# A two-layer graph network on one core: halves of the adjacency matrix fetched and compared at other places of the batch, mirrored blocks first fetched two units sooner

## The chip, the core and the metric

The kernel runs on one core of a Trainium2 chip. The metric is the time of one execution on the device, in microseconds. A run of the kernel before takes 3390.76 us (median of three runs: 3390.57, 3390.76 and 3401.56). Profiles are of one execution each.

## The reference

For 16 graphs of 1024 nodes with 256 features, two layers are computed. Each begins with a layer norm and a ReLU, and each is added to its input:

```
h = relu(layernorm(x));  x = x + L0(h, adj)
h = relu(layernorm(x));  x = x + L1(h, adj)

L0: qkv = layer_norm(h) in 8 heads of 32;  scores = qkv qkv^T / sqrt(32)
    attn = softmax(where(adj > 0, scores, -inf));  h = h + attn qkv
    return h + gelu(layer_norm(h) W1 + b1) W2 + b2
L1: p = h W;  logits = p a_1 + (p a_2)^T + (p a_12) p^T
    e = where(adj > 0, leaky_relu(logits), -9e15)
    return elu(h W_1 + softmax(e) h W_2)
```

Queries, keys and values of L0 are one and the same tensor, so the scores are symmetric. The adjacency matrix is of 32-bit integers and symmetric with ones on the diagonal; the kernel makes use of the symmetry, and it also tests it while it runs.

## The kernel before

All the work is in `fast_path`; `general_path` runs only if a test at the end says so, which is not the case here. A batch is one graph. Nodes are cut into 8 tiles of 128 and into two halves of 512 (`qh` 0 and 1); the 8 heads into two groups of four (`g`).

**Attention of a batch** (`attention`, L984) goes in units. A unit is one group of heads, one half of the queries and one tile of keys. TensorE makes the scores (`s`, L1010), VectorE adds the mask (L1023, two halves of 128x1024), ScalarE takes the exponential and sums it (L1030), and in the next unit TensorE weighs the values (`o`, L1125). For batches from 1 on, 16 units with `qh` 0 come first, then 8 with `qh` 1. For half of the first 16 units, `mirror` (L1040) keeps what the symmetry gives: VectorE transposes the exponentials by 32x32 blocks into `x` (L1046; `xp` has one buffer), SyncE writes them to a DRAM tile `blocks` (L1053), GpSimd adds up their sums (`add_up`, L1059), and SyncE writes these to `rows` (L1074). `gather` (L1084) brings the sums back. In the 8 later units, which this document calls the mirrored stretch, `weigh_mirrored` (L1107) uses 16 blocks that `fetch` (L1093) has read back from DRAM; there are two halves of one buffer (`em`), and block k + 2 is fetched when block k has been used. `em` shares its buffer with the hidden layer `hid` of chunks 0 and 3. Batch 0 computes all 32 units and mirrors nothing.

**Masks.** For each half of a batch, `turn_masks` (L904) loads four row tiles of the adjacency matrix (`fetch_mask`, L587, two loads of 256 KB each into the two buffers `adj`). VectorE converts them to fp8 (`convert_mask`, L594) into `mq`, which has one buffer, and SyncE transposes them by DMA into `mk` (L917; five buffers). `compare_masks` (L924) is the test of symmetry: GpSimd subtracts a part of `mq` from a part of `mk` (`odd`, L932, 4 times for half 0 and 8 times for half 1), and ScalarE squares the difference and sums it into `uneven` (L941). At the end these sums have to be zero.

**The rest of the batch** (`rest`, L1246) is the MLP (`ph`, `po`) and layer 1 (`puT`, `pg`, `lg`, `pa`, `pf`), all by `matmul`, which cuts each product into four column strips (L574) except near the end (L571). The rest of batch b runs between the attention units of batch b + 1. `prologue` (L789) loads and normalizes the next batch.

**What sets the order.** The program is written out in one order by cooperating generators: `stream_a` (attention), `stream_b` (rest), `stream_p`, `stream_c` (prologue), `stream_m` (masks, L1626) and `stream_s`. Each yields a place, a number whose whole part is the batch, and the one with the lowest place goes next. In batches from 1 on a unit with `qh` 0 is 1/25.2 of a batch wide, one with `qh` 1 1.15/25.2. `spread(pieces, n, start, end)` puts pieces at even distances between two places. Beside that, `defer(us, f)` puts a step off until a clock, which counts estimated TensorE time, has advanced by that much. Each engine, and SyncE as the queue of all these DMAs, takes its instructions in the order in which they were written out.

Of the kernel before, what the change touches and what calls it, by code (L numbers as in the profile page):

```python
# [14 lines left out]
AF = mybir.ActivationFunctionType  # L15
ALU = mybir.AluOpType
# [479 lines left out]
def fast_path(  # L496
# [28 lines left out]
    nc = tc.nc  # L525
# [4 lines left out]
    NG = H // GH  # L530
    NT = N // P
# [4 lines left out]
    TPH = QW // P  # L536
# [123 lines left out]
    uneven = const.tile([P, B * 3 * TPH], F32, name="uneven")  # L660
# [111 lines left out]
    def defer(us, f):  # L772
        deferred.append((clock[0] + us, len(deferred), f))

        return clock[0] + us
# [128 lines left out]
    def turn_masks(b, qh, st):  # L904

        ts = list(range(qh * TPH, (qh + 1) * TPH))
        raw = fetch_mask(b, ts[0])
        yield
        m = mkp.tile([P, NT // 2, QW, 2], FP8, tag="mk", name=f"mk_{b}_{qh}")
        st[qh] = m  # L910
        pairs = m.rearrange("p m q r -> p m (q r)").bitcast(BF16)
        mq = st["mq", qh] = mqp.tile([P, TPH, N], FP8, tag="mq", name=f"mq_{b}_{qh}")
        convert_mask(mq[:, 0], *raw)
        raw = fetch_mask(b, ts[1])
        for i in range(TPH):
            yield
            nc.sync.dma_start_transpose(pairs[:, :, i * P : (i + 1) * P], mq[:, i].bitcast(BF16))  # L917
            if i + 1 < TPH:
                convert_mask(mq[:, i + 1], *raw)
            if i + 2 < TPH:  # L920
                raw = fetch_mask(b, ts[i + 2])


    def compare_masks(b, qh, st):  # L924

        for half in range(qh + 1):
            for i in range(TPH):
                kt = qh * TPH + i
                odd = tmpp.tile([P, QW], BF16, tag="w1", bufs=6, name=f"odd_{b}_{qh}_{half}_{i}")
                key = st[half][:, kt // 2, :, kt % 2]  # L930
                query = st["mq", qh][:, i, half * QW : (half + 1) * QW]
                nc.gpsimd.tensor_tensor(  # L932
                    odd.rearrange("p (u v x) -> p u v x", u=2, v=2),
                    key.rearrange("p (u v x) -> p u v x", u=2, v=2),
                    query.rearrange("p (u x v) -> p u v x", u=2, v=2),
                    op=ALU.subtract,
                )
                n = (b * 3 + qh + half) * TPH + i
                defer(
                    3.0,  # L940
                    lambda odd=odd, n=n: nc.scalar.activation(odd, odd, AF.Square, accum_out=uneven[:, n : n + 1]),  # L941
                )
                yield
        if (b, qh) == (B - 1, NQH - 1):
            defer(
                4.0,
                lambda: nc.vector.tensor_reduce(
                    seen[:, 4:5], uneven, axis=mybir.AxisListType.X, op=ALU.add
                ),
            )  # L950
# [33 lines left out]
    def attention(b, st):  # L984
# [6 lines left out]
        blocks = {}  # L991
# [48 lines left out]
        def mirror(g, kt, es):  # L1040
            x = xp.tile([P, NT // 2 * GH, GH, HD], F32, tag="x", name=f"x_{b}_{g}_{kt}")
            if g not in blocks:
                blocks[g] = dramp.tile([NT // 2 * GH, NT // 2 * GH, HD, P], F32, tag=f"blocks{g}", name=f"blocks_{b}_{g}")

            def turn(i):
                nc.vector.transpose(  # L1046
                    x[:, :, 2 * i : 2 * i + 2, :].rearrange("p c h j -> p h c j"),
                    es[i].rearrange("p h (c i) -> p h c i", i=HD),
                )

            def write():
                for a in range(GH):
                    nc.sync.dma_start(  # L1053
                        blocks[g][(kt - TPH) * GH + a].rearrange("c i e -> i c e"),
                        x[a * HD : (a + 1) * HD].rearrange("p c h j -> p c (h j)"),
                    )

            def add_up():
                add = lambda out, p, q: nc.gpsimd.tensor_tensor(out, p, q, op=ALU.add)  # L1059
                part = denp.tile([P, TPH * GH, GH, 8], F32, tag="part", bufs=1, name=f"part_{b}_{g}_{kt}")  # L1060
                add(part, x[:, :, :, 0:8], x[:, :, :, 8:16])
                add(part, part, x[:, :, :, 16:24])
                add(part, part, x[:, :, :, 24:32])
                add(part[:, :, :, :4], part[:, :, :, :4], part[:, :, :, 4:])
                add(part[:, :, :, :2], part[:, :, :, :2], part[:, :, :, 2:4])
                row = denp.tile([P, GH, TPH, GH], F32, tag="row", name=f"row_{b}_{g}_{kt}")
                add(
                    row.rearrange("p a t h -> p t a h"),
                    part[:, :, :, 0].rearrange("p (t a) h -> p t a h", a=GH),
                    part[:, :, :, 1].rearrange("p (t a) h -> p t a h", a=GH),  # L1070
                )
                if ("rows", g) not in blocks:
                    blocks["rows", g] = dramp.tile([TPH, P, GH * TPH * GH], F32, tag=f"rows{g}", name=f"rows_{b}_{g}")
                defer(7.0, lambda: nc.sync.dma_start(blocks["rows", g][kt - TPH], row.rearrange("p a t h -> p (a t h)")))  # L1074

            defer(1.5, lambda: turn(0))
            defer(3.5, lambda: turn(1))
            defer(5.5, write)
            defer(6.5, add_up)

        def gather(g):
# [84 lines left out]
        for n, u in enumerate(units):  # L1166
            qh, g, kt = u
            make_turns()
            es, rest_of_weights = scores(*u)
            go_on()  # L1170
            rest_of_weights()
            first = n == 0 or units[n - 1][:2] != u[:2]
            last = n == len(units) - 1 or units[n + 1][:2] != u[:2]
            scored.append((weigh, (*u, es, first, last)))
            if not mirrored:
                if qh == NQH - 1 and kt % TPH == TPH - 1:
                    invert(kt // TPH, g)
                    if kt < NT - 1:
                        close(kt // TPH, g)
                yield 1.0  # L1180
                continue
            if qh == 0:
                if kt >= TPH:
                    mirror(g, kt, es)
                if n == NG * NT - 1:
                    defer(2.0, lambda: fetch(0))
                    defer(2.2, lambda: fetch(1))
                if n == NT + 1:
                    gather(0)
                if n == NT + 3:  # L1190
                    invert(0, 0)
                    close(0, 0)
                yield 1.0
                continue
            if n == NG * NT + 1:
                gather(1)
            if n == NG * NT + 3:
                invert(0, 1)
                close(0, 1)
            if last:  # L1200
                invert(1, g)
            widths = ((0.8, 0.3, 0.05), (0.5, 0.45, 0.2), (0.4, 0.45, 0.3), (0.3, 0.5, 0.35))[kt - TPH]
            yield widths[0]
            weigh_mirrored(k)
            yield widths[1]
            weigh_mirrored(k + 1)
            k += 2
            yield widths[2]

    def go_on():  # L1210
        if scored:
            f, args = scored.pop()
            f(*args)
        clock[0] += 2.0
# [340 lines left out]
    def spread(pieces, n, start, end):  # L1555
        yield start
        for i, _ in enumerate(pieces):
            yield start + (end - start) * (i + 1) / n

    states = [{} for _ in range(B + 1)]  # L1560
# [65 lines left out]
    def stream_m():  # L1626
        for b in range(B):
            if b:
                start, end = (b - 0.28, b - 0.10) if b == 1 else (b - 0.43, b - 0.25)
                yield from spread(turn_masks(b, 0, states[b]), 5, start, end)  # L1630
                yield from spread(compare_masks(b, 0, states[b]), TPH, end + 0.01, end + 0.09)
                yield from spread(turn_masks(b, 1, states[b]), 5, b + 0.03, b + 0.2)
                yield from spread(compare_masks(b, 1, states[b]), 2 * TPH, b + 0.21, b + 0.36)
            else:
                yield from spread(compare_masks(b, 0, states[b]), TPH, b + 0.02, b + 0.2)
                yield from spread(turn_masks(b, 1, states[b]), 5, b + 0.23, b + 0.43)
                yield from spread(compare_masks(b, 1, states[b]), 2 * TPH, b + 0.52, b + 0.7)
# [85 lines left out]
```

## Time and profile before

| | before |
|---|---|
| median of three runs | 3390.76 us |
| the profiled execution | 3397.68 us |
| its span | 3395.4 us |
| TensorE busy (mean granted clock 0.988) | 3239.8 us, 95% |
| VectorE busy | 2584.0 us, 76% |
| ScalarE busy | 2205.2 us, 65% |
| GpSimd busy | 1515.3 us, 45% |
| TensorE waiting for `em`, at L1107 | 64.5 us |
| the ACTIVATE of L941: 192 times, mean | 625 ns |
| L932: 192 times, mean | 1165 ns |
| L594: 248 times, mean | 562 ns |

In the views of the profile PE is TensorE, PEld its loading of weights, DVE VectorE, ACT ScalarE, POOL GpSimd and SP SyncE. Busy time is the time in which at least one instruction of an engine ran. A wait is the idle time of an engine just before an instruction, named after what ended it. A line is the line of the kernel; a helper's line stands for all its callers, so tiles are given too. A group is all instructions of one line, operation and tile; "x240" is how many there were. A window is a piece of the span, in microseconds from its start.

### The profile page before, as it was taken

How to read it: one execution, taken by the hardware profiler on the slowest of the kernel's cores; microseconds unless marked ns; L12 is line 12 of the kernel's file. 1: busy time of each engine (PE TensorE's matmuls, PEld its weight loads, DVE VectorE, ACT ScalarE, POOL GpSimd, SP SyncE). 2: the span in 40 equal slices, each digit the busy share in tenths (PEclk: the TensorE clock that was granted, in tenths of full speed). 3: DMA queues.
4: the chain of work that ended last, by engine and by line, in shares of the span. 5: the costliest groups of instructions: out<-in, count | busy, mean ns of one | idle time of the engine just before them, and what ended most of it. 6: DMA issues, size and time to landing. Idle time of an engine off the chain costs nothing. (4 is left out here: it accounts for less than half of the span.)

```text
span 3395.4 us, 114970 instructions
## 1 busy us (share of the span) xinstructions
PE 3239.8 (95%) x48866; PEld 1600.2 (47%) x48866; DVE 2584.0 (76%) x4881; ACT 2205.2 (65%) x5384; POOL 1515.3 (45%) x1757
## 2 busy tenths in 40 slices
PE   6899999999999999999999999999999999999998
PEld 2244445444444444444444454444544444444477
DVE  5677787777888778787787887778877787877734
ACT  6875756758567585665757567585675856758553
POOL 3563543635436364453635436354362543636120
PEclk9999999999999999999999999999999999999999
DMA  5256454454654455555455544645445464444410
GB/s 136 69 112 141 114 134 128 102 150 116 141 131 109 131 120 133 132 119 128 109 147 123 135 121 110 150 115 136 126 104 141 114 144 127 109 130 113 119 36 14
DMA packets 741161, 404.82 MB, mean 119 GB/s; under 512 B 173217, under 2 KB 699937, under 8 KB 740641
## 3 DMA queue, kind: packets, MB, share of 16 engines
q1 hardware_dynamic: 740352, 397.14, 48.0%
q8 instruction: 386, 6.32, 0.8%
q14 instruction: 135, 1.10, 0.1%
q10 hardware_dynamic: 288, 0.26, 0.0%
HBM read 233.97 MB, written 146.54 MB: 112 GB/s over the span
## 5 line engine op out<-in xcount | busy, mean ns | idle before, releaser
L1030 ACT ACTIVATE e<-e 128x512 f32<-128x512 f32 x1504 | 929.5, 620 | 496.6 <-DVE e L1023 493.2
L1023 DVE TENSOR_TENSOR e<-s,mk 128x1024 f32<-128x1024 f32 x752 | 885.2, 1217 | 197.5 <-PE s L1010 182.8
L574 PE MATMUL lg<-fT,uT 128*32 128x256 f32 x7680 | 471.1, 392 | 0.0
L574 PE MATMUL ph<-yT,w 128*32 128x256 f32 x7808 | 443.3, 380 | 7.0 <-DVE yT L1292 7.0
L574 PE MATMUL pa<-gw,e 128*32 128x258 f32 x7584 | 446.1, 380 | 0.0
L1010 PE MATMUL s<-kT 32*64 32x512 f32 x6272 | 442.1, 614 | 0.9 <-DVE e L1023 0.9
L574 PE MATMUL po<-w,hid 128*32 128x256 f32 x7680 | 434.4, 379 | 0.0
L1125 PE MATMUL o<-e,va 128*32 128x512 f32 x3136 | 422.5, 606 | 0.4 <-ACT e L1030 0.4
L574 PEld LDWEIGHTS lg<-fT,uT 128*32 128x32 f32 x7680 | 255.8, 113 | 211.0 <-issue 48.4
L574 PEld LDWEIGHTS ph<-yT,w 128*32 128x32 f32 x7808 | 250.5, 110 | 210.4 <-issue 29.0
L1046 DVE STREAM_TRANSPOSE x<-e 128x1024 f32<-128x1024 f32 x240 | 293.7, 1239 | 73.0 <-ACT e L1030 44.4
L574 PEld LDWEIGHTS po<-w,hid 128*32 128x32 f32 x7680 | 250.0, 110 | 202.8 <-issue 45.2
L574 PEld LDWEIGHTS pa<-gw,e 128*32 128x32 f32 x7584 | 246.0, 110 | 185.5 <-issue 22.1
L1409 DVE SCALAR_TENSOR_TENSOR e<-lg,gw,mk 128x256 f32<-128x256 f32 x512 | 223.5, 478 | 125.9 <-PE lg L574 114.9
L1059 POOL TENSOR_TENSOR part<-part,x 128x512 f32<-128x512 f32 x240 | 310.3, 1293 | 18.8
L1415 ACT ACTIVATE e<-e,shift 128x512 f32<-128x512 f32 x256 | 183.5, 717 | 159.8 <-DVE e L1414 149.0
L1030 ACT ACTIVATION_READ_ACCUMULATOR e<-e 128x1 f32 x1504 | 283.4, 188 | 0.0
L1059 POOL TENSOR_TENSOR part<-x 128x512 f32<-128x512 f32 x120 | 156.5, 1304 | 230.4 <-DVE x L1046 224.6
L829 POOL TENSOR_TENSOR nrm<-nrm,g 128x256 f32<-128x256 f32 x128 | 110.8, 865 | 312.3 <-DVE nrm L749 312.3
L745 POOL TENSOR_TENSOR rs_c<-ve_c,mhalf 128x2 f32<-128x2 f32 x64 | 44.7, 699 | 421.0 <-DVE ve_c L743 421.0
L932 POOL TENSOR_TENSOR odd<-mk,mq 128x512 bf16<-128x512 fp8e5 x192 | 220.8, 1165 | 25.2 <-DMA mk<-mq 25.2
L1316 ACT ACTIVATE hid<-ph,b1c 128x256 f32<-128x256 f32 x512 | 204.9, 465 | 41.0 <-PE ph L574 26.5
(145 smaller groups left out, 4430.7 us busy)
## 6 DMA issues: line engine op xcount, KB each, us to landing
blocks<-x SPq DMA_DIRECT2D x480, 256.0 KB, 4.6
em<-blocks SPq DMA_DIRECT2D x240, 512.0 KB, 4.3
adj<-in_adj_dram SPq DMA_DIRECT2D x248, 256.0 KB, 4.0
h<-in_x_dram SPq DMA_DIRECT2D x64, 256.0 KB, 3.0
xb<-in_x_dram SPq DMA_DIRECT2D x128, 128.0 KB, 3.5
out_dram<-z SPq DMA_DIRECT2D x128, 128.0 KB, 4.0
rows<-row SPq DMA_DIRECT2D x120, 32.0 KB, 2.8
gather<-rows SPq DMA_DIRECT2D x120, 32.0 KB, 3.1
```

Source lines behind the costliest of these rows:

```text
L574: nc.tensor.matmul(out[c : c + HD], lhsT[:, c : c + HD], rhs, start=start, stop=stop)
L829: nc.gpsimd.tensor_mul(nrm, nrm, g1)
L932: nc.gpsimd.tensor_tensor(odd.rearrange("p (u v x) -> p u v x", u=2, v=2), key.rearrange("p (u v x) -> p u v x", u=2, v=2), query.rearrang ...
L1010: nc.tensor.matmul(sc[j // 2][c : c + P // 2, j % 2, :], kT[r, g, kt * P + c : kt * P + c + P // 2], kT[r, g, qs], start=j >= by_pe, stop= ...
L1023: nc.vector.tensor_tensor(e, masked, mb, op=ALU.add)
L1030: nc.scalar.activation(e[:, j], masked[:, j], AF.Exp, scale=SCALE, accum_out=sums[kt // TPH, g][:, n, kt % TPH, qh : qh + 1],)
L1046: nc.vector.transpose(x[:, :, 2 * i : 2 * i + 2, :].rearrange("p c h j -> p h c j"), es[i].rearrange("p h (c i) -> p h c i", i=HD),)
L1059: add = lambda out, p, q: nc.gpsimd.tensor_tensor(out, p, q, op=ALU.add)
L1125: nc.tensor.matmul(o[j * HD : (j + 1) * HD, :], va[:, kt, (g * GH + j) * HD : (g * GH + j + 1) * HD], es[j // 2][:, j % 2, :], start=first ...
L1316: nc.scalar.activation(hid[:, f0 + i, :], ph[:, i, :], AF.Identity, bias=b1c[:, f0 + i : f0 + i + 1])
L1409: nc.vector.scalar_tensor_tensor(e[:, j, :], lg[:, j, :], gw[:, kt, D : D + 1], st[c // 2][:, kt // 2, qs, kt % 2], op0=ALU.add, op1=ALU.add,)
L1415: ready = defer(2.5, lambda: nc.scalar.activation(e, e, AF.Exp, bias=shift))
```

## The change

There are four edits. The mask streams get other places: half 0 of batches from 2 on is fetched and turned at 0.27 to 0.40 of the batch before, where it was 0.57 to 0.75, and compared at 0.41 to 0.50, where it was 0.76 to 0.84; half 1 is turned at 0.02 to 0.16 of its own batch (0.03 to 0.20) and compared at 0.17 to 0.26 (0.21 to 0.36). Batch 0 and the start of half 0 of batch 1 stay. The difference of half 1 is now reduced by VectorE (largest absolute value) and not squared and summed by ScalarE; half 0 stays with ScalarE. The write of `rows` is put off by 10 and not by 7. The first two fetches of mirrored blocks are issued in the unit n = 13 and not n = 15.

```diff
                 n = (b * 3 + qh + half) * TPH + i
-                defer(
-                    3.0,
-                    lambda odd=odd, n=n: nc.scalar.activation(odd, odd, AF.Square, accum_out=uneven[:, n : n + 1]),
-                )
+
+                def collect(odd=odd, n=n):
+                    if qh == 0:
+                        nc.scalar.activation(odd, odd, AF.Square, accum_out=uneven[:, n : n + 1])
+                    else:
+                        nc.vector.tensor_reduce(
+                            uneven[:, n : n + 1], odd, axis=mybir.AxisListType.X, op=ALU.max, apply_absolute_value=True
+                        )
+
+                defer(3.0, collect)
                 yield
...
-                defer(7.0, lambda: nc.sync.dma_start(blocks["rows", g][kt - TPH], row.rearrange("p a t h -> p (a t h)")))
+                defer(10.0, lambda: nc.sync.dma_start(blocks["rows", g][kt - TPH], row.rearrange("p a t h -> p (a t h)")))
...
-                if n == NG * NT - 1:
+                if n == NG * NT - 3:
                     defer(2.0, lambda: fetch(0))
                     defer(2.2, lambda: fetch(1))
...
-                start, end = (b - 0.28, b - 0.10) if b == 1 else (b - 0.43, b - 0.25)
+                start, end = (b - 0.28, b - 0.10) if b == 1 else (b - 0.73, b - 0.60)
                 yield from spread(turn_masks(b, 0, states[b]), 5, start, end)
-                yield from spread(compare_masks(b, 0, states[b]), TPH, end + 0.01, end + 0.09)
-                yield from spread(turn_masks(b, 1, states[b]), 5, b + 0.03, b + 0.2)
-                yield from spread(compare_masks(b, 1, states[b]), 2 * TPH, b + 0.21, b + 0.36)
+                yield from spread(compare_masks(b, 0, states[b]), TPH, end + 0.01, end + 0.10)
+                yield from spread(turn_masks(b, 1, states[b]), 5, b + 0.02, b + 0.16)
+                yield from spread(compare_masks(b, 1, states[b]), 2 * TPH, b + 0.17, b + 0.26)
```

## The prediction

> **What bounds the kernel now.** I read the page first: TensorE is busy 3239.8 us of the 3395.4 us span (95%), no other engine over 76%. So only what TensorE loses can be won, some 155 us with the start and the end. Its own waits come next (engine, line, releaser: us in total, times, longest):
>
> ```profile
> PE o L1107 <- DMA em<-blocks: 64.5, 21, 5.2
> PE ptk L837 <- POOL va L830: 19.2, 5, 15.1
> PE o L1107 <- DVE os L1134: 11.0, 12, 1.0
> ```
>
> The first line is weigh_mirrored (L1107) waiting for the block that fetch (L1093) brings back from DRAM. The second is the start of the program. Where does the first one fall? I cut one batch into its first stretch (16 units, qh 0 with mirroring) and its mirrored stretch (8 units, qh 1), and the last batch likewise (columns: us; PE, PEld, DVE, ACT, POOL busy; clock; DMA share; GB/s):
>
> ```profile
> 1181.00:1305.00 124.00, 122.70 (x1916) 58.09 (x1912) 99.29 (x174) 92.44 (x221) 74.49 (x86) 1.00 0.49 115
> 1305.00:1389.00 84.00, 78.12 (x1236) 39.18 (x1228) 63.95 (x134) 43.93 (x112) 23.00 (x26) 0.96 0.55 142
> 3165.00:3240.00 75.00, 75.00 (x1248) 37.85 (x1240) 56.09 (x109) 38.57 (x100) 8.25 (x11) 1.00 0.50 138
> ```
>
> The first stretch is full. The mirrored one loses 6 us and has a clock of 0.96. The last batch, which has no next batch and so no masks to fetch and no prologue to run, does even more matmuls in 75 us without a gap. SyncE's order of time in the stretch with the loss (start, duration):
>
> ```profile
> 1303.72 1.01 SPq L1093 DMA_DIRECT2D em<-blocks  x2
> ...
> 1311.05 1.69 SPq L587 DMA_DIRECT2D adj<-in_adj_dram  x2
> 1312.83 0.39 SPq L1093 DMA_DIRECT2D em<-blocks  x1
> 1313.27 1.26 SPq L917 DMA_TRANSPOSE mk<-mq  x1
> 1315.58 1.68 SPq L587 DMA_DIRECT2D adj<-in_adj_dram  x2
> 1317.30 2.14 SPq L1084 DMA_DIRECT2D gather<-rows  x4
> 1319.56 2.12 SPq L1093 DMA_DIRECT2D em<-blocks  x2
> ```
>
> and TensorE's:
>
> ```profile
> 1318.09 0.64 PE L1107 MATMUL o<-em,va 128*32 128x256 f32 x8 [0.54 <-DMA em<-blocks]
> ...
> 1324.67 1.08 PE L1107 MATMUL o<-em,va 128*32 128x256 f32 x8 [4.20 <-DMA em<-blocks]
> 1325.52 3.64 PE L574 MATMUL lg<-fT,uT 128*32 128x256 f32 x32
> ```
>
> The buffer of block 3 was free at about 1312.9, when the second L1107 group had run, but its fetch left at 1319.56: between stand a transpose, two adj loads (which wait until VectorE has converted the tile before) and the gather. It landed 5.1 us later. The same picture stands in 14 batches (1 to 14). And the 32 matmuls behind it took 3.64 us where 1.91 is usual. The clock column over 2 us steps shows why:
>
> ```profile
> 1324.00:1326.00 2.00, 1.33 (x16) 0.65 (x20) 0.00 (x0) 0.00 (x0) 1.84 (x4) 0.50 1.17 246
> 1326.00:1328.00 2.00, 2.00 (x24) 0.94 (x20) 0.00 (x0) 0.00 (x0) 0.38 (x1) 0.50 0.34 72
> ```
>
> **What the skill says.** The Trainium skill, "TensorE: Matmul & The Clock Gate", section "What's actually happening": after an idle window of about 3.4 us the clock falls to half until a window of activity has passed. The trace agrees: 0.50 after a gap of 4.2 us. The same page, "Architectural detail", says that VectorE, ScalarE and GpSimd are strict FIFOs; so an instruction that waits holds all behind it. The trace agrees in its L1046 waits for POOL (26.0 us in 14 waits, with VectorE's later work behind). "VectorE: DVE Perf Modes", "The perf-mode tier table", has tensor_reduce in its plain mode only, for bf16 too; the trace has one 128x512 tensor_reduce, of f32, 0.64 us. "GPSIMD Engine Reference", "Key points": POOL shares its SBUF interfaces with VectorE; here the conversions of L594 run from 0.38 to 1.51 us.
>
> **The change part by part.** Durations are of the profiled run: 3395.4 us of span, 3397.7 us in all; that is 6.9 above the median of the three shown, 3390.8.
>
> *1. Half 0 of batches 2 to 15 moves* from places 0.57 to 0.75 of the batch before (comparison to 0.84) to 0.27 to 0.40 (comparison to 0.50). The mirrored stretch starts at unit 16 of width 25.2, place 0.635, so this takes the four transposes, four of the eight adj loads (two more leave just ahead of it) and three of the four pairs of conversions out of it. Batch 1's stay at 0.72, but batch 0 has no mirrored stretch. With SyncE clear, fetch 3 follows the gather alone: free at 1312.9, gather of 2.1 us done by about 1315, landing after 4.3 (page, part 6) at 1319.3; TensorE wants it at 1318.1 + 0.43 + 1.74 = 1320.3. The last batch shows just this order without a wait. What goes: the 64.5 us, of which I let 5% stay, so **-61**. The half clock: (1 - clock) over the 8 to 9 us after each of the 14 long waits sums to 30.6 us (seven of 1.5 to 1.7, seven of 2.2 to 3.0). It goes with the gaps: **-29**. The os wait (11.0, and 2.6 of the same kind behind nrm) comes of VectorE being about a microsecond behind; one pair of conversions (0.8 to 1.1 us) leaves just ahead of it. Between 0 and -13.6; I take **-6**. Next late in that stretch is nothing that the last batch shows, so TensorE is the bound again.
>
> *2. What the first stretch takes in.* VectorE there has 99.3 of 124 us. It gets at most 8 conversions x 0.56 (L594's mean) = 4.5 us, and 8 reductions x 0.64 = 5.1: 108.9, or 88%. POOL gets 4 subtractions x 1.165 = 4.7 on 74.5. The rows are:
>
> ```profile
> L932 POOL TENSOR_TENSOR odd<-mk,mq 128x512 bf16<-128x512 fp8e5 x192 | 220.8, 1165 | 25.2 <-DMA mk<-mq 25.2
> L594 DVE TENSOR_SCALAR mq<-adj 128x512 fp8e5<-128x512 int32 x248 | 131.4, 562 | 25.3 <-DMA adj<-in_adj_dram 24.9
> L941 ACT ACTIVATE odd<-odd 128x512 bf16<-128x512 bf16 x192 | 119.9, 625 | 66.9 <-POOL odd L932 66.9
> L727 DVE TENSOR_REDUCE seen<-sq 128x1 f32<-128x512 f32 x1 | 0.6, 644 | 0.0
> ```
>
> ScalarE loses 8 x (0.625 + 0.19) = 6.5 us a batch there and gets 4 x 0.81 = 3.3 from half 0. None of this is on the path by itself: TensorE's o of a unit comes a whole unit (7.8 us) after its s, while mask addition (2.36), exponentials (3.3) and their start need about 6. It counts by queueing. The eight subtractions of half 1 go from 0.21-0.36 (31 us) to 0.17-0.26 (19 us), where POOL also has one add_up per two units (5.8 us) and the residual additions (1.5 a pair). Following batch 7's order (unit 4 at 1416, unit 6 at 1431): three subtractions run before the add_up of 1426.5 to 1432.2; the fourth comes behind it and behind two residual additions, done at 1434.8. Its reduction, due 3 us after issue, stands on VectorE from 1429.8: a wait of some 5 us, and ahead of unit 6's mask addition (L1023, 1432.2 today). The addition then ends at 1437.8 to 1439, the exponentials at 1440 to 1441, and TensorE's o is due at 1441.7: just in time; yT and unit 7 behind it would be 0.5 to 2 us late. VectorE's idle time from 1430 to 1464 is now 13 us, against 7 of new work and 5 of waiting. Bounds: nothing, if the 13 us absorb it (below nothing too: ScalarE is freed of 104 us in all, and waits of 66.9 leave it), and 5 us a batch, if the whole wait is passed on. I take 1.5 us in 15 batches: **+22**.
>
> *3. First refills two units sooner* (unit 13 for 15): no L1107 waits for blocks 0 and 1 today; the first group waits for os. They pass one write of blocks and one of rows on SyncE, and need hid's buffer, whose last reader (contract 3) ends at 1476, before unit 13 at 1488. **0**; cover gone, it would cost a landing, 4.3 us.
>
> *4. rows written 3 us later* (7 to 10): SyncE waits 159 us in 61 waits at L1074 for POOL; some 3 us less each, hidden. The gather reads rows about 22 us after the mirror, so it isn't passed. **0**, with a gather wait of up to 2.4 us (its longest now) as the other end.
>
> Sum: -61 - 29 - 6 + 22 = **-74**: 3397.7 to 3324 on the profiled run, 3317 from the median. I say **3322**, since a second run of the three was also high.
>
> **Rivals.** (a) *Free of charge*: the first stretch swallows it all and os goes too: -95.1 - 13.6 = -109, 3282 (from the median) to 3289 (profiled run). For it: the stretch's clock of 1.00. Against: VectorE at 88% in strict order. (b) *The crowd takes much of it*: 3.5 us of TensorE a batch, +52: -44, 3347 to 3354 (3345 to 3374 with 3 to 4.5 us). For it: the working of part 2; against: ScalarE's relief. (c) *Slower*: VectorE behind POOL at the reductions. If a batch's eight waits sum past VectorE's 13 us less 7 of new work, the rest reaches TensorE; when a gap passes about 3 us the half clock adds 1.7 to 2.8. 6.5 + 2.3 us in 15 batches is +132 against -96 won: 3427 from the median. It decides from 6.4 us a batch. Against: today's wait behind POOL is 2.5 us at its longest. (d) *The fetch stays late*, because gather and em still queue behind one another: half of the 95 stays: -48 - 6 + 22 = -32, 3359 to 3366. Against: the last batch.
>
> **How the numbers follow.** Forecast 0.60 (3300 to 3345), a 0.10, b 0.15, c 0.09, d 0.06. A measurement of this kernel can tell about 0.5%, 17 us. Faster: forecast, a, most of b, half of d: 0.85; same 0.06; slower 0.09. The range 3290 to 3370 leaves out c, half of a and some of b and d, together 0.18.
>
> **What would show it.** Right: the em wait of L1107 under 10 us; clock 1.00 in mirrored stretches, which last 77 to 78 us; adj loads and transposes absent there; first stretches of 124 to 127 us; 128 reductions near 0.64 us at the subtraction's line and 64 squares. Wrong: VectorE waiting for POOL odd by more than 5 us a batch, with TensorE idle before o or s in units 5 to 8; a clock under 1 in first stretches; or em waits that stay.

## The result and the profile after

| | before | after |
|---|---|---|
| median | 3391.99 us (4 runs) | 3365.53 us (4 runs, 3361.70 to 3368.62) |
| ratio after to before, 95% interval | | 0.9916 (0.9894 to 0.9937) |
| the profiled execution | 3397.68 us | 3366.83 us |
| its span | 3395.4 us | 3365.1 us |
| TensorE busy | 3239.8 us | 3249.6 us |
| VectorE busy | 2584.0 us | 2688.1 us |
| ScalarE busy | 2205.2 us | 2123.7 us |

By the medians the change makes the kernel 26.5 us faster; by the ratio it is 0.84%, and the interval leaves out 1. The forecast was -74 us. What was to go went; what came in its place is larger than forecast.

TensorE's own waits after (engine, line, releaser: us in total, times, longest):

```profile
PE ptf L1367 <- DVE mv_a L741: 28.7, 9, 3.9
PE ptk L837 <- POOL va L830: 19.0, 5, 15.3
PE ptf L1367 <- ACT ft L765: 13.4, 5, 3.2
```

The wait for `em`, 64.5 us before, is not on the list any more, nor is the one for `os`. A wait that was not forecast is in their place: `ptf`, the transposing of layer 1's input, 42.1 us in 14 waits. Before it was short:

```profile
PE ptf L1361 <- ACT ft L765: 6.8, 9, 1.3
```

The stretches of batch 6, cut at the same instructions as before's windows (us; PE, PEld, DVE, ACT, POOL busy; clock; DMA share; GB/s):

```profile
1172.35:1299.13 126.78, 123.99 (x1916) 58.17 (x1912) 110.30 (x189) 90.25 (x214) 79.50 (x90) 1.00 0.57 132
1299.13:1374.40 75.27, 75.06 (x1236) 38.56 (x1228) 61.48 (x127) 41.20 (x104) 18.15 (x22) 1.00 0.45 125
```

The counts of matmuls are those of before (1916 and 1236), so the cut is the same. The mirrored stretch goes from 84.0 to 75.3 us, without a gap and at clock 1.00. The first stretch goes from 124.0 to 126.8 us, and VectorE in it from 99.3 to 110.3.

SyncE in the mirrored stretch of that batch (start, duration):

```profile
1303.95 0.39 SPq L1099 DMA_DIRECT2D em<-blocks  x1
1304.45 3.40 SPq L1090 DMA_DIRECT2D gather<-rows  x4
1307.95 5.78 SPq L1099 DMA_DIRECT2D em<-blocks  x3
```

No adjacency load and no transpose stands between the fetches, only the gather. On TensorE the groups of L1113 (the old L1107) follow without a bracket, which is where a wait would be printed:

```profile
1310.52 0.61 PE L1113 MATMUL o<-em,va 128*32 128x256 f32 x8
1310.94 1.93 PE L574 MATMUL pa<-gw,e 128*32 128x258 f32 x32
1312.69 0.61 PE L1113 MATMUL o<-em,va 128*32 128x256 f32 x8
```

**The lengths of the units.** Waits name only who came last, so I took the distance from the first score matmul of one unit to that of the next, in each batch, and the mean over batches 2 to 14. In all the other units of the 24, before and after agree within 0.1 us.

| units | before | after | difference |
|---|---|---|---|
| 6, 7, 8 (reductions) | 23.97 | 25.82 | +1.85 |
| 9, 10 | 15.61 | 15.66 | +0.05 |
| 11, 12 (half 0 just turned, `ptf` waits) | 17.63 | 20.94 | +3.31 |
| 16, 17 (`em` waits) | 26.78 | 18.70 | -8.08 |
| all 24 | 207.50 | 204.57 | -2.93 |

Over the program, with the same sums for batches 1 and 15: units 16 and 17 give -112.4, units 11 and 12 +47.9, units 6 to 8 +26.7. The rest is small: +2.5 in units 0 to 3 of batch 1, +1.1 in its units 10 and 13, +1.8 before it, +2.6 behind the last attention unit. The sum is -29.8; the spans differ by -30.3.

**Where units 11 and 12 lose.** VectorE in units 9 to 11 of batch 8 of the kernel after (a bracket gives the idle time ahead of an instruction and what ended it):

```profile
1647.76 1.33 DVE L594 TENSOR_SCALAR mq<-adj 128x512 fp8e5<-128x512 int32 x1 [0.30 <-DMA adj<-in_adj_dram]
1649.43 1.08 DVE L594 TENSOR_SCALAR mq<-adj 128x512 fp8e5<-128x512 int32 x1 [0.34 <-DMA adj<-in_adj_dram]
1650.43 2.34 DVE L1029 TENSOR_TENSOR e<-s,mk 128x1024 f32<-128x1024 f32 x2
...
1661.65 1.25 DVE L1052 STREAM_TRANSPOSE x<-e 128x1024 f32<-128x1024 f32 x1 [2.41 <-ACT e L1036]
1663.73 0.43 DVE L740 BATCH_NORM_STATS2 st_a<-h 128x6 f32<-128x256 f32 x1 [0.83 <-DMA h<-in_x_dram]
1668.68 2.34 DVE L1029 TENSOR_TENSOR e<-s,mk 128x1024 f32<-128x1024 f32 x2
```

ScalarE at the end of unit 11:

```profile
1672.45 0.61 ACT L942 ACTIVATE odd<-odd 128x512 bf16<-128x512 bf16 x1
1672.97 0.19 ACT L942 ACTIVATION_READ_ACCUMULATOR odd<-odd 128x1 f32 x1
1673.06 1.08 ACT L765 ACTIVATE ft<-xb,nm_d,rs_d 128x256 f32<-128x256 f32 x2
```

and TensorE, with the scores of unit 11 at its head:

```profile
1662.72 1.11 PE L1016 MATMUL s<-kT 32*64 32x512 f32 x16
...
1673.70 0.93 PE L1367 MATMUL ptf<-ident,ft 128*128 128x128 f32 x4 [3.12 <-DVE mv_a L741]
1674.56 2.01 PE L1016 MATMUL s<-kT 32*64 32x512 f32 x16
```

The scores of the same unit and their mask addition before:

```profile
1678.68 1.11 PE L1010 MATMUL s<-kT 32*64 32x512 f32 x16
...
1681.75 2.34 DVE L1023 TENSOR_TENSOR e<-s,mk 128x1024 f32<-128x1024 f32 x2
```

A pair of conversions (L594) waits for its loads and runs 1.33 and 1.08 us where the median is 0.43, so the mask addition of unit 9 starts 3.3 us after its scores (1.2 before). Its exponentials are late in turn, and ScalarE's work behind them, and then the transpose of unit 10, first in VectorE's queue, waits 2.41 us for ScalarE, and the prologue's statistics (`st_a`) wait 0.83 us for `h`. In unit 11 the mask addition starts 5.96 us after the scores; before it was 3.07 (means over batches 2 to 14: 5.78 and 3.80). `ft`, which `ptf` transposes, stands on ScalarE behind those exponentials and, new in this place and in each of the 14 batches, behind a square of half 0's comparison (L942). TensorE waits 3.12 us, and `ptf` starts at 1673.70, when the first of the two `ft` is done. The bracket names VectorE's `mv_a`, which is one of several releasers; the order of time shows that it is `ft`, as the second `ptf` line of the waits has it. After the gap the clock goes down and the next 16 score matmuls take 2.01 us where 1.11 is usual:

```profile
1674.00:1676.00 2.00, 1.94 (x20) 0.53 (x18) 1.90 (x6) 2.00 (x5) 1.97 (x3) 0.66 0.48 140
1676.00:1678.00 2.00, 2.00 (x16) 0.40 (x12) 1.48 (x3) 0.87 (x4) 2.00 (x4) 0.50 0.02 6
```

Between 230 and 3240 us the clock is at half for 3.41 us, or for twice that, at a time: before behind each of the 14 long `em` gaps (seven times 3.41, seven times 6.83), after behind 12 of the 14 `ptf` gaps (ten times 3.41, twice 6.83). (1 - clock) sums to 35.8 us before and 23.9 after: two thirds of the half clock moved from the `em` gaps to the `ptf` gaps.

**The reductions**, by their line (shortest, median and longest in ns; then who kept VectorE idle ahead of them: us, times):

```profile
L944 DVE TENSOR_REDUCE uneven<-odd x128: 635/676/689, 89.1 to 3068.8; 128x1 f32<-128x512 bf16 x128
its engine sat idle before it (us, times) until:
  POOL odd L932: 70.5, 44
```

A reduction costs 0.68 us, and VectorE stands idle for 70.5 us in front of them, 4.4 a batch, with its later work behind.

### The profile page after: what moved, and what is told of

Same layout as the page of the kernel before. It is cut to its first block, busy times and chain, and to the rows that moved or that the text cites. A ratio compares the mean times of both kernels' runs of the same rounds, so it can differ in the third digit from the quotient of the medians.

```text
span 3365.1 us, 114909 instructions
## 1 busy us (share of the span) xinstructions
PE 3249.6 (97%) x48866; PEld 1602.6 (48%) x48866; DVE 2688.1 (80%) x5009; ACT 2123.7 (63%) x5128; POOL 1517.0 (45%) x1757
## 3 DMA queue, kind: packets, MB, share of 16 engines
q14 instruction: 135, 1.11, 0.1%
## 5 line engine op out<-in xcount | busy, mean ns | idle before, releaser
L1016 PE MATMUL s<-kT 32*64 32x512 f32 x6272 | 464.2, 629 | 0.5 <-DVE e L1029 0.5
L574 PE MATMUL lg<-fT,uT 128*32 128x256 f32 x7680 | 450.3, 379 | 0.3 <-ACT gw L1397 0.3
L1131 PE MATMUL o<-e,va 128*32 128x512 f32 x3136 | 435.8, 617 | 0.0
L574 PEld LDWEIGHTS lg<-fT,uT 128*32 128x32 f32 x7680 | 248.8, 110 | 198.2 <-issue 27.2
L829 POOL TENSOR_TENSOR nrm<-nrm,g 128x256 f32<-128x256 f32 x128 | 100.5, 785 | 344.2 <-DVE nrm L749 344.2
```

The source lines that it names most:

```text
L574: nc.tensor.matmul(out[c : c + HD], lhsT[:, c : c + HD], rhs, start=start, stop=stop)
L1016: nc.tensor.matmul(sc[j // 2][c : c + P // 2, j % 2, :], kT[r, g, kt * P + c : kt * P + c + P // 2], kT[r, g, qs], start=j >= by_pe, stop= ...
L1131: nc.tensor.matmul(o[j * HD : (j + 1) * HD, :], va[:, kt, (g * GH + j) * HD : (g * GH + j + 1) * HD], es[j // 2][:, j % 2, :], start=first ...
```

## Experiments

Theory 1: the missing 47 us come of two crowds in the first stretch. Half 0's conversions and loads, now in units 9 to 11, push back mask additions, transposes and the prologue's first statistics, so `ft` and `ptf` are late; the reductions cost a smaller part by making VectorE wait for GpSimd. Theory 2: the reductions are the whole cost, and the `ptf` waits are what they leave behind. Theory 3: half 0's comparison, with GpSimd waiting up to 10.2 us for a mask, is what delays the chain. (The expectation of e1 puts this under its theory 1.)

All kernels below are told by the median of four runs or more and by the ratio to the kernel before on the same chip (whose median was 3392.0 us beside the kernel after, 3398.2 us in the first eight below it and 3397.2 us in the last four). The lengths are in us, means over batches 2 to 14:

| kernel | median | ratio (95%) | units 6-8 | 9-10 | 11-12 | 16-17 | 19 | 21 | all 24 |
|---|---|---|---|---|---|---|---|---|---|
| before |  |  | 23.97 | 15.61 | 17.63 | 26.78 | 10.00 | 8.98 | 207.50 |
| after | 3365.5 | 0.9916 (0.9894 to 0.9937) | 25.82 | 15.66 | 20.94 | 18.70 | 10.01 | 8.98 | 204.57 |
| e1_compare_late | 3359.4 | 0.9892 (0.9875 to 0.9908) | 25.96 | 15.65 | 20.13 | 18.72 | 10.00 | 8.98 | 203.99 |
| e2_half0_back | 3418.3 | 1.0056 (1.0039 to 1.0073) | 25.84 | 15.61 | 16.87 | 27.01 | 10.01 | 8.98 | 208.72 |
| e3_places_only | 3351.0 | 0.9865 (0.9849 to 0.9882) | 24.43 | 15.61 | 21.30 | 18.71 | 10.01 | 8.98 | 203.47 |
| e4_half0_end | 3374.5 | 0.9935 (0.9918 to 0.9951) | 26.27 | 15.61 | 16.89 | 18.76 | 10.00 | 11.81 | 204.95 |
| f1_half0_mid_squares | 3308.6 | 0.9734 (0.9718 to 0.9750) | 24.46 | 15.62 | 16.88 | 18.81 | 11.43 | 8.98 | 200.62 |
| f2_reduce_later | 3350.5 | 0.9855 (0.9838 to 0.9871) | 24.13 | 15.70 | 21.77 | 18.72 | 10.01 | 8.98 | 203.70 |
| f3_convert_twice | 3429.2 | 1.0084 (1.0067 to 1.0101) | 26.07 | 18.70 | 22.32 | 18.73 | 10.01 | 8.98 | 209.31 |
| f4_rows_fetch_only | 3398.6 | 1.0000 (0.9992 to 1.0009) | 23.97 | 15.61 | 17.71 | 26.76 | 10.01 | 8.98 | 207.44 |
| g1_prologue_later | 3318.7 | 0.9765 (0.9749 to 0.9782) | 25.83 | 15.67 | 17.60 | 18.01 | 10.01 | 9.57 | 201.18 |
| g2_half0_mid_alone | 3309.6 | 0.9735 (0.9719 to 0.9751) | 23.97 | 15.61 | 17.86 | 18.81 | 11.42 | 8.98 | 201.11 |
| g3_half0_wide | 3324.5 | 0.9785 (0.9769 to 0.9801) | 24.54 | 15.61 | 16.88 | 20.09 | 10.38 | 8.98 | 201.48 |
| g4_half0_sooner | 3304.1 | 0.9726 (0.9709 to 0.9742) | 24.33 | 15.61 | 16.88 | 18.72 | 11.23 | 8.98 | 200.23 |

### e1: half 0's comparison later (from the kernel after)

```diff
-yield from spread(compare_masks(b, 0, states[b]), TPH, end + 0.01, end + 0.10)
+yield from spread(compare_masks(b, 0, states[b]), TPH, *((end + 0.01, end + 0.10) if b == 1 else (b - 0.33, b - 0.20)))
```

> The changed kernel, with the four subtractions and squares of half 0 put into the mirrored stretch (places 0.67 to 0.80 for 0.41 to 0.50); loads, conversions and transposes stay. Theory 1 (half 0's work in the first stretch makes the normalized tile ft of chunk 2 late): POOL no longer waits 10 us for the last transpose there and ScalarE no longer has a square ahead of ft, so the ptf wait falls from about 3.0 to 1.8 us a batch and the half clock behind it goes: about 3323 us, and POOL's wait for mk under 20 us. Theory 2 (the reductions of half 1, behind POOL, are what costs): no change, 3365 us.

TensorE's waits:

```profile
PE ptf L1367 <- DVE st_a L740: 23.3, 8, 3.4
PE ptf L1367 <- ACT ft L765: 10.7, 6, 2.2
```

The `ptf` wait falls from 42.1 to 34.0 us, units 11 and 12 only from 20.94 to 20.13. The expectation had the wait at about 1.8 us a batch and the time at 3323 us; they are 2.4 and 3359.4. So the comparison of half 0 has about 0.8 us a batch of the loss, about what the square in front of `ft` takes, and not the rest: theory 3 falls as the main cause. The intervals of the two ratios, of this kernel and the one after, overlap, so the time alone would not tell them apart.

### e2: half 0 back at its old places (from the kernel after)

```diff
-start, end = (b - 0.28, b - 0.10) if b == 1 else (b - 0.73, b - 0.60)
+start, end = (b - 0.28, b - 0.10) if b == 1 else (b - 0.43, b - 0.25)
```

> The changed kernel with half 0 back at its old places (0.57 to 0.75); half 1, the reductions, rows and the earlier first fetches stay as changed. Theory 1: the em waits of about 64 us and their half clock of about 30 return, the ptf wait falls below 1 us a batch: 3385 to 3400 us. Theory 2: the em waits return and the reductions' cost stays on top: 3410 to 3430 us.

```profile
PE o L1113 <- DMA em<-blocks: 66.2, 25, 4.9
...
PE o L1113 <- DVE os L1140: 13.1, 14, 1.0
```

The `em` and `os` waits are back in full and no `ptf` wait is on the list; units 11 and 12 fall to 16.87. So it is the move of half 0 that makes both the gain and the new wait. The time lies in the range that the expectation has under theory 2, since the reductions' cost stays on top, while the `ptf` waits go as under theory 1: both costs are there. What stays of the change costs 20.1 us over before: units 6 to 8 take 1.87 us more a batch, from the reductions and the denser places of half 1, and units 11 and 12 give back 0.76. These units take 16.87 to 16.89 in every kernel that has half 1 at its new places and half 0 elsewhere (e2, e4, f1, g3, g4), and 17.6 to 17.9 with half 1 at its old ones (before, f4, g2). So half 0's own cost there is 20.94 - 16.87 = 4.07 us a batch.

### e3: only the places change (from the kernel after)

```diff
-if qh == 0:
+if qh >= 0:
...
-defer(10.0, lambda: nc.sync.dma_start(blocks["rows", g][kt - TPH], row.rearrange("p a t h -> p (a t h)")))
+defer(7.0, lambda: nc.sync.dma_start(blocks["rows", g][kt - TPH], row.rearrange("p a t h -> p (a t h)")))
...
-if n == NG * NT - 3:
+if n == NG * NT - 1:
```

> Only the places of the mask streams are changed; squares all on ScalarE, rows after 7, first fetches in unit 15, as before. Theory 1: the ptf wait stays at 3 us a batch or grows, since ScalarE has 6.5 us more a batch: 3365 to 3385 us. Theory 2: without reductions the loss goes: about 3330 us.

```profile
PE ptf L1367 <- ACT ft L765: 24.9, 9, 3.5
...
PE ptf L1367 <- DVE mv_a L741: 18.1, 5, 4.4
```

With squares on ScalarE for both halves, units 6 to 8 go from 25.82 to 24.43, and the `ptf` wait stays at 43.0 us. So theory 2 falls: without a single reduction the new wait is there in full. The time, 3351.0, lies between the two that were expected, as units 6 to 8 get shorter. The reductions have 1.39 of the 1.85 us in units 6 to 8, the denser places of half 1 the other 0.46.

### e4: half 0 at the end of the batch (from the kernel after)

```diff
-start, end = (b - 0.28, b - 0.10) if b == 1 else (b - 0.73, b - 0.60)
+start, end = (b - 0.28, b - 0.10) if b == 1 else (b - 0.25, b - 0.08)
...
-yield from spread(compare_masks(b, 0, states[b]), TPH, end + 0.01, end + 0.10)
+yield from spread(compare_masks(b, 0, states[b]), TPH, end + 0.01, end + 0.09)
```

> The changed kernel with half 0 at the end of the mirrored stretch (places 0.75 to 0.92, compared at 0.93 to 1.01). Theory 1: the first stretch is rid of half 0, ptf waits under 1 us a batch, and behind the gather SyncE has 5 us of room per refill, so em waits are short: 3300 to 3315 us. If SyncE's order holds the refills up again wherever masks lie beside them, em waits of 30 to 60 us return: 3360 to 3390 us. Theory 2: 3365 us or a little less.

```profile
PE o L1113 <- DMA em<-blocks: 28.6, 15, 4.3
PE ph L574 <- DVE yT L1298: 23.6, 32, 3.1
```

SyncE at the start of unit 21 of batch 6, and TensorE in units 20 and 21:

```profile
1339.27 1.15 SPq L587 DMA_DIRECT2D adj<-in_adj_dram  x2
1340.51 1.01 SPq L1099 DMA_DIRECT2D em<-blocks  x2
```

```profile
1335.57 0.62 PE L1113 MATMUL o<-em,va 128*32 128x256 f32 x8
...
1345.86 0.64 PE L1113 MATMUL o<-em,va 128*32 128x256 f32 x8 [1.87 <-DMA em<-blocks]
```

The time that I hoped for, 3300 to 3315 us, did not come. Units 11 and 12 are as short as in e2 and units 16 and 17 as short as after, so both losses are gone at once. But a later refill now stands behind a pair of the same loads: its buffer was free at about 1336.2, it left at 1340.51, and unit 21 waits for it (11.81 for 8.98), and the comparison now runs into the next batch and delays `yT` in unit 0 (11.14 for 10.08). The kernel needs half 0 in the mirrored stretch behind the refills of units 16 and 17 and ahead of the one of unit 21.

### f1: half 0 between these, squares for both halves (from the kernel after)

```diff
-if qh == 0:
+if qh >= 0:
...
-start, end = (b - 0.28, b - 0.10) if b == 1 else (b - 0.73, b - 0.60)
+start, end = (b - 0.28, b - 0.10) if b == 1 else (b - 0.30, b - 0.15)
...
-yield from spread(compare_masks(b, 0, states[b]), TPH, end + 0.01, end + 0.10)
+yield from spread(compare_masks(b, 0, states[b]), TPH, *((end + 0.01, end + 0.10) if b == 1 else (b - 0.14, b - 0.06)))
```

> The changed kernel with squares for both halves on ScalarE and half 0 in the mirrored stretch behind the gather (places 0.70 to 0.85, compared at 0.86 to 0.94). Theory 1 (per batch: 8 us won in units 16 and 17 by freeing SyncE between the gather and the second pair of refills; 3.3 lost in units 11 and 12 to half 0; 1.7 to 1.9 lost in units 6 to 8 to the reductions): units 16 and 17 stay short, 11 and 12 are back at 17.6 us, 7 and 8 at 14.5; if no refill is late further on, 200 us a batch, which is 3290 to 3305 us; with one late refill of 2.8 us a batch, about 3335. If the refills are late wherever masks lie near them: over 3370.

```profile
PE o L1113 <- DMA em<-blocks: 17.0, 14, 2.0
```

Units 16 and 17 stay short, units 11 and 12 too, and unit 21 is back at 8.98. Left are 17.0 us of waits, in unit 19, of 2.0 us at most, behind which the trace has no half clock. With the losses of the first stretch all but gone (units 6 to 8 keep 0.5 us) and nearly all of the gain kept, the time is 13 us under the forecast, and 4 over the range of its own expectation.

### f2: the reductions wait less (from the kernel after)

```diff
-defer(3.0, collect)
+defer(9.0 if qh else 3.0, collect)
...
-4.0,
+10.0,
```

(The second edit puts off the last reduction of `uneven` in the same way.)

> The changed kernel with the eight reductions of half 1 put off by 9 us after the subtraction and not 3. If the cost in units 6 to 8 is VectorE waiting behind POOL, these units fall from 25.8 to about 24.1 us, VectorE's wait for odd from 70 us to under 15, and the time by some 25 us to about 3340; if it is the reductions' own 0.68 us each, nothing changes: 3365.

```profile
PE ptf L1367 <- DVE mv_a L741: 31.2, 9, 4.3
...
PE ptf L1367 <- ACT ft L765: 14.5, 5, 3.7
```

VectorE's wait for `odd`, 70.5 us after, is not on this kernel's list. Units 6 to 8 fall from 25.82 to 24.13, with the same 128 reductions on VectorE. So the reductions cost by waiting in front of GpSimd and not by their 0.68 us each, which is the mechanism that the prediction named. Units 11 and 12 grow by 0.83 us, and the `ptf` waits stay; so the time falls to 3350.5 and not to the 3340 expected.

### f3: each conversion of half 0 done twice (from the kernel after)

```diff
+twice = qh == 0 and b > 1
...
-convert_mask(mq[:, 0], *raw)
+for _ in range(1 + twice):
+    convert_mask(mq[:, 0], *raw)
...
-convert_mask(mq[:, i + 1], *raw)
+for _ in range(1 + twice):
+    convert_mask(mq[:, i + 1], *raw)
```

> The changed kernel with each conversion of half 0 done twice (8 more of about 0.43 us a batch). If VectorE's work there is what makes ft late, units 11 and 12 grow by 1.5 us a batch or more (21 to 22.5 us and over): 3385 to 3400 us. If it is SyncE's order or a DMA (adj, h) that is late, they grow by less than 0.5: under 3375 us.

```profile
PE ptf L1370 <- DVE mv_a L741: 46.7, 12, 4.4
...
PE s L1019 <- DVE e L1032: 10.4, 15, 2.7
```

Eight conversions more a batch make units 9 to 12 longer by 18.70 - 15.66 + 22.32 - 20.94 = 4.42 us. In all they keep VectorE busy for 240.5 - 171.0 = 69.5 us more in these 14 batches, 5.0 a batch. The busy share would have left VectorE room for them (110.3 of 126.8 us in the first stretch of batch 6), but nearly all of them reach TensorE. Most of it comes in units 9 and 10 (3.04); units 11 and 12 grow by 1.38, just under the 1.5 that was expected, and the time is 29 us over the expected range.

### f4: the other two edits alone (from the kernel before)

```diff
-defer(7.0, lambda: nc.sync.dma_start(blocks["rows", g][kt - TPH], row.rearrange("p a t h -> p (a t h)")))
+defer(10.0, lambda: nc.sync.dma_start(blocks["rows", g][kt - TPH], row.rearrange("p a t h -> p (a t h)")))
...
-if n == NG * NT - 1:
+if n == NG * NT - 3:
```

> The kernel before with only the two small edits: rows written after 10 and first fetches in unit 13. Both theories: no unit changes by more than 0.3 us; within 5 us of the kernel before. If SyncE blocked at rows or the early refills matter by themselves: 10 us or more either way.

The ratio is 1.0000 (0.9992 to 1.0009) in 12 runs. The later `rows` and the earlier first refills do nothing by themselves.

### g1: the prologue later (from the kernel after)

```diff
-yield from spread(prologue(b, states[b]), 28, b - 0.600, b - 0.150)
+yield from spread(prologue(b, states[b]), 28, b - 0.520, b - 0.120)
```

> The changed kernel with the next batch's prologue (loads of h, its statistics and normalization, mostly VectorE's work) begun at 0.48 of the batch and not 0.40. Half 0 stays in the first stretch. If ft is late because VectorE has too much ahead of it in units 9 to 11, whatever the work is, taking the prologue's first statistics away shortens units 11 and 12 by 1 us or more together (21 to under 20 us): 3340 to 3352 us, if it doesn't come back later in the prologue. If it is half 0's DMAs and the subtractions' wait alone, less than 0.5 us changes: about 3365.

VectorE in unit 11 of batch 8, whose scores start at 1634.72 in this kernel, and TensorE's `ptf` there:

```profile
1635.87 1.24 DVE L1052 STREAM_TRANSPOSE x<-e 128x1024 f32<-128x1024 f32 x1
...
1639.05 2.34 DVE L1029 TENSOR_TENSOR e<-s,mk 128x1024 f32<-128x1024 f32 x2
```

```profile
1644.07 0.93 PE L1367 MATMUL ptf<-ident,ft 128*128 128x128 f32 x4 [1.48 <-ACT ft L765]
```

More than expected. The mask addition stands 4.3 us after the scores (5.96 in the kernel after), the `ptf` wait here is 1.48 us for 3.12, in all 13.3 us in 12 waits, and units 11 and 12 take 17.60, as before (17.63). Half 0, its loads and the reductions are where the change put them. So most of the loss in these units, 3.34 of 4.07 us, comes of half 0 and the prologue meeting there, and it goes when either leaves. Of the waits that remain only one, of 2.14 us, has half clock behind it. The edit moves the prologue's loads and its work on ScalarE and GpSimd too; that VectorE is the place of the meeting rests on the order of time above and on f3.

### g2: one line (from the kernel before)

```diff
-start, end = (b - 0.28, b - 0.10) if b == 1 else (b - 0.43, b - 0.25)
+start, end = (b - 0.28, b - 0.10) if b == 1 else (b - 0.30, b - 0.15)
```

> The kernel before with one line changed: half 0 at places 0.70 to 0.85. Half 1, squares, rows and first fetches stay as before. Theory: all of the gain lies in clearing SyncE between the gather and the second pair of refills; units 16 and 17 fall from 26.8 to about 18.8 us, unit 19 takes 1.4 more, the rest stays: 6.6 us in 14 batches, about 3305 us. If the earlier half 1 was needed for it: over 3330.

```profile
PE o L1107 <- DMA em<-blocks: 17.7, 17, 2.5
```

As expected: 3309.6 us with half 0 alone moved, behind the critical refills. Nothing else of the change is needed.

### g3: half 0 wider (f1 with other places)

```diff
-start, end = (b - 0.28, b - 0.10) if b == 1 else (b - 0.30, b - 0.15)
+start, end = (b - 0.28, b - 0.10) if b == 1 else (b - 0.32, b - 0.12)
...
-(b - 0.14, b - 0.06)
+(b - 0.11, b - 0.03)
```

> As the version with half 0 at 0.70 to 0.85 and squares, but at 0.68 to 0.88. If the wait in unit 19 goes with wider spacing: 200.6 less 1.4 us a batch, about 3290 us; if it only moves: 3300 to 3320.

Missed: the time is over both ranges. The wait of unit 19 shrinks (10.38), but unit 17 grows (10.96) and the later comparison costs unit 0 (10.64 for 10.06), in all more than it gives.

### g4: half 0 a unit sooner (f1 with other places)

```diff
-start, end = (b - 0.28, b - 0.10) if b == 1 else (b - 0.30, b - 0.15)
+start, end = (b - 0.28, b - 0.10) if b == 1 else (b - 0.34, b - 0.17)
...
-(b - 0.14, b - 0.06)
+(b - 0.16, b - 0.08)
```

> The same at 0.66 to 0.83, so that the first load stands near the gather again. If the gather and the loads in one unit are what makes the refill late, unit 17 grows again by 3 us or more: 3340 us or over; if two units' distance from the old place is enough: about 3300.

```profile
PE o L1113 <- DMA em<-blocks: 13.2, 13, 1.6
```

The fastest of all: 3304.1 us, ratio 0.9726 (0.9709 to 0.9742). Half 0's loads don't delay the gather or the refill behind it: units 16 and 17 take 18.72. Against f1 (0.9718 to 0.9750) and g2 the intervals overlap, so these three are one result: half 0 in the mirrored stretch, a little later than it was.

## Why the prediction was right or wrong

**Step 1, right, and a little small.** Its three terms come to -96 us; units 16 and 17 gave -112.4. The `em` wait is gone where 5% was left standing, the half clock there with it, and the `os` wait too, of which I had taken about half. Before's own terms sum to 64.5 + 30.6 + 13.6 = 108.7; the 30.6 leaves out the end of the longer stretches at half clock, with which it is 35.8. The reading of SyncE's order was right: e2, which puts the loads and transposes back ahead of the fetch, brings the wait back, and e3 and f4 show that the earlier first refills have no part in the gain.

**Step 2, wrong: +22 in the sum, 26.7 + 47.9 = 74.6 measured.** This term has two halves, and only one was priced.
- The reductions were given all of the 22, 1.5 us a batch, and cost 26.7 together with the denser places of half 1. Mechanism and size held: f2 takes the wait for GpSimd away and keeps the work, and 1.69 of the 1.85 us a batch go; by e3 the reductions have 1.39.
- Half 0's own work in the first stretch was given nothing: "None of this is on the path by itself", and what was to cover it was "VectorE's idle time from 1430 to 1464 is now 13 us". That step failed; units 11 and 12 cost 47.9 us. The idle time was summed over 34 us, but VectorE takes its work in order, and its idle time lies in waits for others: for the scores, for the exponentials. Conversions stood ahead of mask additions, as in unit 9 of batch 8, and did not fall into that time. They also got longer: the mean of L594 went from 562 to 714 ns (131.4 to 171.0 us in all). 156 of the 248 now run beside an instruction of GpSimd, where 88 did, and these take 889 ns in the mean, the others 417. Its waits for loads went from 24.9 to 47.4 us. I followed the order of one batch by hand only to unit 8; the damage of half 0 is in units 11 and 12, behind the start of the next batch's prologue (place 0.40, unit 10), of whose work there the prediction says nothing. e3 shows that the loss is there without the reductions, f3 that it grows with the conversions, e2, e4 and f1 that it goes when half 0 leaves, and g1 that most of it goes when the prologue does.

The same strict order that I cited from the Trainium skill, "TensorE: Matmul & The Clock Gate", "Architectural detail", and used for the reductions, held for the conversions: the transpose that waited 2.41 us held the statistics and the next mask addition behind it.

**The half clock** was counted as won for good, at -29. It is bound to gaps and not to a place: 14 new gaps of 2.1 to 3.9 us brought two thirds of it back, 23.9 us for 35.8.

**Steps 3 and 4, right at nothing,** by f4, on the kernel before.

**The rivals.** (b), the crowd takes much of it, had the right place, the first stretch. Its 3.5 us a batch were laid to the working of part 2, the reductions, and were too low in all, 74.6 / 15 = 5.0, and too high for these. Its wider range, 3345 to 3374, holds the measured time; by its own sum, with 3 to 4.5 us, it should have been 3340 to 3369, which does too. (c), slower, needed 6.4 us a batch, so the cost came near it in size; but VectorE behind GpSimd at the reductions, its cause, has only the smaller part. (d), 3359 to 3366, has the measured time in it by luck: no fetch is late. (a), 3282 to 3289, was reached by no kernel; f1, g2 and g4, with half 0 at other places, come to 3304 to 3310, between it and the forecast.

**What would show it.** The mirrored stretch was to last 77 to 78 us and took 75.3; the first stretch, 124 to 127, took 126.8 in batch 6. That is one of the milder batches: units 11 and 12 lost 1.4 us there, and between 1.1 and 5.3 elsewhere. VectorE's wait for `odd` was to stay under 5 us a batch and is 4.4. One sign of being wrong came true, a clock under 1 in first stretches: the half clock behind 12 of the `ptf` gaps. TensorE idle in units 11 and 12 was not on my list, which had units 5 to 8. Of ScalarE's 66.9 us of waits in front of squares, which were to go with the reductions, 40.0 are left, in front of half 0's.

What stays open: the 2.6 us behind the last attention unit and the 4.3 us up to unit 3 of batch 1, which no run followed up, and how the loss in units 11 and 12 divides between longer conversions, later loads and the order on VectorE.

## What to carry to other kernels

Idle time of an engine that works in order need not be room: before counting moved work as covered, follow the order through every unit in which it lands and a few beyond, and name what else starts there. When a load blocks a queue, moving it a little behind the critical transfer (one line here, -2.65%) can be better than moving it to a stretch that is full. To see what a change did, compare the lengths of the same unit in both kernels; gains and losses that cancel in the time stand apart there.

## What the runs showed of the hardware that was not expected

The conversion from int32 to fp8 of 128x512 on VectorE took 0.38 to 1.52 us in the kernel after. Where no instruction of GpSimd ran beside it, it took at most 0.43 us, in all fourteen kernels; every longer one ran beside GpSimd. So its mean rose by 27% (562 to 714 ns) when it was put at other times, and in g4, where 62 of the 248 run beside GpSimd, it is 609 ns.

A tensor_reduce of 128x512 bf16 to its largest absolute value took 0.68 us, against 0.67 us for the f32 one of that size in the same kernel: bf16 was no faster.

The prediction takes from the Trainium skill, "TensorE: Matmul & The Clock Gate", "What's actually happening", an idle window of about 3.4 us before the half clock. Here shorter gaps were enough: in the kernel after one of 2.15 us (before `ptf` at 1879 us) had half clock behind it, and one of 2.46 us (at 2699 us) had none. So the length of a gap does not decide it alone; where page and measurement differ, the measurement stands.
